# Attention over sorted edges: k and q[dst] both kept in SBUF, one block more ahead, and the weighing behind the logits

## The chip, the cores and the metric

The kernel runs on one core of one Trainium2 chip. The metric is the device time of one execution in microseconds, the median of several runs. The five engines of the core take their instructions each from a queue of its own and meet by semaphores: TensorE (PE, matrix products and transposes, into PSUM), VectorE (DVE), ScalarE (ACT), GpSimd (POOL, here the indirect loads) and SyncE (SP, here the other loads and stores).

## The reference, cut to what matters

There are N = 12500 nodes and E = 212500 edges of F = 128 numbers each, in 8 heads of 16. The edges come sorted by dst.

```
h = relu(layernorm(x))
q = h @ Wq.T + bq
k = edge_attr @ Wk.T + bk
v = h @ Wv.T + bv
qs, qd = q[src], q[dst]
in_m   = sum(qs * k)      # per edge and head
out_m  = sum(qd * k)
diag_m = sum(qs * qd)
att = edge_weight ** lam
score = (softmax_by_dst(in_m / 4) + softmax_by_dst(out_m / 4) + softmax_by_dst(diag_m / 4)) * att
out = x + leaky_relu(segment_sum(score * v[dst], dst) @ Wo.T + bo, 0.1)
```

So each edge needs the rows q[src], q[dst] and k, three products of them summed over a head, and then a softmax over the edges of one dst.

## The kernel before

The kernel first computes q for all nodes into a table in DRAM (some 160 us), then runs a loop over blocks of 512 edges, and ends with the output of the last nodes. The loop has 415 blocks. They belong to five streams, each a fifth of the sorted edges: block g is of stream s = g % 5 and turn t = g // 5, so a turn is five blocks, one of each stream. A block is four tiles of 128 edges (`JN` = 4).

For each block, in the order of the code:

- `gather` (GpSimd, L696): four indirect loads of q[src] into the tile `qq`, `LOOK` = 23 blocks ahead of their use, in `QQ` = 25 buffers. Each waits, besides its buffer, for a TensorE product noted in `behind`.
- `spread_q` (TensorE, L1201): since the edges are sorted, the dst of a block lie in a window of 38 nodes. One-hot columns (`oh`) times the window's rows of q (`win`, kept as three bf16 terms) give q[dst] in one half of the PSUM tile `kq_ps`, and the bias of k in the other half. `kq_ps` has two buffers of two banks each.
- `project` (TensorE, L1190): the turned edges `eT` times Wk are added to k's half of `kq_ps`. Behind it ScalarE copies the half with q[dst] to the SBUF tile `qd` (L1194).
- `turn` (TensorE, L1183): the next edges are transposed into `eT_ps` (one buffer), and ScalarE copies them to `eT` (L1185).
- `logits` (VectorE): q[dst] times k (L1215, from `qd` and `kq_ps`), then q[src] times both halves of `kq_ps` (L1216), into the tile `prod`. After the blocks s = 0, 2 and 4 the sums over the heads follow (L1220, of one block or of two) into `lT`.
- `one_hots` (ScalarE, L1177 and L1178): makes `oh` from the loaded positions `relb`.

Once per turn, spread over its five blocks, the work on the logits of earlier turns runs: `turn_logits` (L1241, transposes into `l_ps`), scans along the edges that give the maximum of each dst (L1274, L1279, L1292), `turn_max` (L1366, back into `m_ps`), `powers` at s = 3 (VectorE subtracts the maximum, L1376, and ScalarE takes the exponential, L1377, in the tile `back`), `show_ends` at s = 3 (L1402, L1405, L1406: the matrix `sel` of which edge belongs to which node), `weigh_powers` at s = 4 (VectorE, L1387: powers times the edges' weights, into the other half of `back`), and `to_rows` at s = 4 (L1417: `sel` times `back` into `w_ps`, and ScalarE's copy L1423). SyncE loads a turn's edges with one DMA (`fetch_edges`, L684, into `ea`, two buffers), its positions (`fetch_places`, L641, `relb`), the windows (`fetch_rows`, L650), the marks of the ends (`fetch`, L627, `far`), and stores the rows (`put_rows`, L1434). The class `Nodes` puts the output work of finished nodes between.

The order on each engine is fixed by hand: `pin` chains each instruction to the one that the code issued before it on the same engine. So the order of the lines in the loop is the order of work, and an instruction that waits holds all behind it on its engine. In block g the loop spreads and projects block g + 1, turns block g + 2, makes the one-hot columns of block g + 3 and multiplies block g.

Of the kernel before, what the change touches and what calls it, by code (L numbers as in the profile page):

```python
# [7 lines left out]
F32 = mybir.dt.float32  # L8
# [464 lines left out]
def ordered_path(ctx: ExitStack, tc: tile.TileContext, flag, x, src, dst, edge_attr, edge_weight,  # L473
# [19 lines left out]
    nc = tc.nc  # L493
    N, F = x.shape
    E = src.shape[0]
    P = 128
    NI = -(-N // P)
    NP = P * NI
    BE, JN = 512, 4
# [11 lines left out]
    H3 = 3 * HEADS  # L511
# [75 lines left out]
    worst = consts.tile([RW, 1], F32, name="worst")  # L587
    LEAD, RAW, AHEAD = 3, 15, 11
    raw_i = consts.tile([P, LEAD, S, JN], I32, name="raw_i")
    LOOK, QQ, BEGIN = 23, 25, 12  # L590
    end = S * G
    edges = ctx.enter_context(ExitStack())
    gath = edges.enter_context(tc.tile_pool(name="gath", bufs=QQ))
# [4 lines left out]
    def pin(inst):  # L598

        engine = str(inst.ins.engine)  # L600
        if engine in pinned:
            tc.add_manual_dep(inst.ins, pinned[engine], mybir.DependencyInfo(
                mybir.DependencyClass.NoSync, mybir.DependencyReason.DATA), reason="in order")
        pinned[engine] = inst.ins.name
        return inst
# [8 lines left out]
    qqs, st, eas, behind, base_v, places = {}, {}, {}, {}, {}, {}  # L614
# [29 lines left out]
    def fetch_rows(t, of=range(S)):  # L644
        if t >= G:
            return
        if 0 in of:
            st[t]["win"] = wins[t % 2]
        for s in of:
            win = pin(nc.sync.dma_start(st[t]["win"][:, s, :],  # L650
                                        q3_table[bass.ds(base_v[t][s] * 3, K3), :]))
            apart(win, [term_stores[u] for u in units_of(s, t)])
# [28 lines left out]
    def fetch_edges(t):  # L681
        if t < G:
            ea = eas[t] = load.tile([P, S, JN * F], F32, name="ea")
            pin(nc.sync.dma_start(  # L684
                ea, edge_attr[:end * BE, :].rearrange("(s b p j) f -> p s b (j f)", s=S, b=G, p=P)
                [:, :, t, :]))
# [52 lines left out]
    with tc.tile_pool(name="prep", bufs=1) as prep, \  # L739
# [44 lines left out]
        rest = E - (RW - 1) * RC  # L784
# [280 lines left out]
    class Nodes:  # L1065
# [39 lines left out]
        def turn(self, to):  # L1105
            for b in range(self.n):
                pin(nc.tensor.transpose(to[:, b, :], self.h[:, b, :], ident))
            if self.hT is None:
                self.hT = fin.tile([P, JN, P], F32, name="hT")
            pin(nc.scalar.copy(self.hT[:, :self.n], to[:, :self.n]))  # L1110
# [50 lines left out]
    with tc.tile_pool(name="work", bufs=2) as work, \  # L1161
            tc.tile_pool(name="scan", bufs=2) as scan, \
            tc.tile_pool(name="ps", bufs=1, space=PSUM) as ps:
        kqs, eTs, qds, ohs, lTs, prods = {}, {}, {}, {}, {}, {}

        def banks_of(g):

# [4 lines left out]
        def one_hots(g):  # L1172

            if g < end:
                oh = ohs[g] = work.tile([K3, BE], BF, name="oh", bufs=5)
                d = places[g // S][:K3, g % S, :]
                pin(nc.scalar.activation(d, d, AF.Abs, bias=before[:K3]))  # L1177
                pin(nc.scalar.activation(oh, d, AF.Relu, bias=1.0, scale=-1.0))  # L1178
# [9 lines left out]
        def project(g):  # L1188
            for j in range(JN):
                pin(nc.tensor.matmul(kqs[g][:, j, 1, :], eTs[g][:, j, :], wk, start=False,  # L1190
                                     stop=(j % 2 == 1)))
            del eTs[g]
            qds[g] = work.tile([P, JN, F], F32, name="qd")
            pin(nc.scalar.copy(qds[g], kqs[g][:, :, 0, :]))  # L1194

        def spread_q(g):

            s, win = g % S, st[g // S]["win"]
            kq = banks_of(g)
            for j in range(JN):  # L1200
                pin(nc.tensor.matmul(kq[:, j].rearrange("p i f -> p (i f)"),  # L1201
                                     ohs[g][:, j * P:(j + 1) * P], win[:, s:S + 1:S - s, :],
                                     start=(j % 2 == 0), stop=False))
            del ohs[g]

        def logits(g):
            s, t = g % S, g // S
            if s == 0:
                lTs[t] = scan.tile([P, JN, S, H3], F32, name="lT", bufs=3)
            alone = t == G - 1 and s > 2  # L1210
            lo = s if alone else max(0, s - 1 + s % 2)
            if s == lo:
                prods[0] = work.tile([P, JN, 2, 3, F], F32, name="prod", bufs=1)
            prod = prods[0][:, :, s - lo]
            pin(nc.vector.tensor_mul(prod[:, :, 2, :], qds[g], kqs[g][:, :, 1, :]))  # L1215
            pin(nc.vector.tensor_mul(prod[:, :, 0:2, :],  # L1216
                                     qqs[g][:, :, None, :].to_broadcast([P, JN, 2, F]),
                                     kqs[g]))
            if s % 2 == 0 or alone:
                pin(nc.vector.tensor_reduce(  # L1220
                    lTs[t][:, :, lo:s + 1, :].rearrange("p j s c -> p j (s c)"),
                    prods[0][:, :, :s + 1 - lo].rearrange("p j s i (h d) -> p j (s i h) d", d=DIM),
                    AX.X, ALU.add))
            del kqs[g], qds[g], qqs[g]

        last = {}
        ends_ab = scan.tile([P, len(rest) * JN, 2, 2 * H3], F32, name="ends_ab", bufs=1)
        for i in range(2):
            ends_t.append(scan.tile([K4, P], BF, name=f"ends_t{i + 2}", bufs=1))
            nc.vector.memset(ends_t[-1][0:1, :], 1.0)  # L1230
# [1 line left out]
        def small(shape, name):  # L1232
            return ps.tile(shape, F32, name=name, tag="small", bufs=3)
# [286 lines left out]

        products = str(mybir.EngineType.PE)
        leaving, last_pair = pairs[G - 3], pairs[G - 1]
        fetch_rows(0)
        fetch(1)
        fetch_places(1)
# [5 lines left out]
        turn(1)  # L1531
        one_hots(1)
        one_hots(2)
        for g in range(end):
            s, t = g % S, g // S
            nodes_before(t, s)
            gather(g + LOOK)
            if s == 0:
                fetch_edges(t + 1)
            if g + 1 < end:  # L1540
                spread_q(g + 1)
                behind[g + 1, 0] = pinned[products]
                project(g + 1)
                behind[g + 1, 1] = pinned[products]
            if g + 2 < end:
                turn(g + 2)
                behind[g + 1, 2] = pinned[products]
            if s == 4:
                later(weigh_powers, t - 2)
            logits(g)  # L1550
            if s == 3:
                later(powers, t - 2)
            one_hots(g + 3)
            if s == 0:
                if t > 0:
                    turn_logits(t - 1)
                later(select, t - 2)
                later(spread_far, t - 2)
            elif s == 1:
                later(scan_on, t - 1)  # L1560
                later(scan_back, t - 2)
                if t == 1:
                    logits_few()
            elif s == 2:
                if t == G - 2:
                    show_ends(G - 1)
                later(turn_max, t - 2)
                fetch_places(t + 2)
            elif s == 3:
                later(show_ends, t - 2)  # L1570
                fetch(t + 2)
            elif t < G - 1:
                later(to_rows, t - 2)
            ahead, k = (t + 2, s - 3) if s > 2 else (t + 1, s + 2)
            if ahead > 1:
                fetch_rows(ahead, [k])
            if g < end - 1:
                later(put_rows, t - 2 if s == 4 else t - 3, [(s + 1) % S])
            if t == G - 3 and 0 < s < 3:
                select(G - 2 + s)  # L1580
            if t == G - 2 and s == 4:
                show_ends(G)
            if t == G - 1 and s == 0:
                select(G - 2)
            if t == G - 1 and s == 4:
                show_ends(G - 2)
            behind[g + 1, 3] = pinned[products]
            nodes_between(t, s)
            other_terms(t, s)
            if g == 12 * S:  # L1590
                examine()
            begin_rest(g - (end - BEGIN))
            if g == end - 2:
                hold(rest[0], True)
            if g == end - 1:
                last_pair.turn(small([P, JN, P], "node_ps"))
                more_banks()
            if g < S:
                of = [u for u in range(NU) if g in parts_of(u)]
                pin(nc.scalar.dma_start(  # L1600
                    sums[g][of[0] * UN:(of[0] + len(of)) * UN].rearrange(
                        "(n p) i c -> p n (i c)", p=P),
                    blank[:, None, :].to_broadcast([P, 2 * len(of), 2 * 2 * H3])))
# [28 lines left out]
        hold(rest[1])  # L1632
        last_pair.turn(small([P, JN, P], "node_ps"))
        last_pair.project_o(small([P, JN, F], "node_ps"))
        for r, of in enumerate(rest):
            of.load_sums(ends_ab[:, r * JN:r * JN + of.n], of.more)
        last_pair.take_larger()
# [88 lines left out]
```

## Time and profile before

| what | us |
|---|---|
| three runs, median (lowest to highest) | 2659.78 (2658.79 to 2670.84) |
| the profiled execution, its own time | 2642.74 |
| its span, first to last instruction | 2640.9 |
| TensorE products, busy | 1657.0 (63%) |
| TensorE weight loads, busy (beside products) | 1406.9 (53%) |
| VectorE busy | 2002.2 (76%) |
| ScalarE busy | 1422.5 (54%) |
| GpSimd busy | 1587.3 (60%) |
| mean granted TensorE clock | 0.786 |
| moved by DMA | 355.74 MB, 135 GB/s on average |

The costliest groups of instructions besides those shown in the prediction, with their total, the mean of one, and the engine's idle time just before them:

```
L1190 TensorE  kq_ps, 4 a block      x3320  627.3 us, 348 ns   677.0 us idle before
L1220 VectorE  sums over the heads   x250   702.3 us, 2809 ns    8.5 us
L1185 ScalarE  copy of eT            x415   244.5 us, 589 ns   174.8 us
L1177 ScalarE  one-hot, first part   x415   301.8 us, 727 ns     0.0 us
L1178 ScalarE  one-hot, second part  x415   261.5 us, 630 ns    13.2 us
```

A matmul on f32 operands is shown as two passes, so 4 tiles of 415 blocks are 3320 records at L1190. Busy time is an average over the span. Which engine is waited for is read from the idle times before the groups and from the chain of waits, which follows the work that ended last back to the start. A waiter's releaser "remote" is one that the profile could not tie to an instruction. Ends of matmuls are modelled, not measured.

### The profile page before, as it was taken

The page shows a single profiled execution, that of the slowest core. Times are in us where ns is not written, and L with a number is a line of the kernel's source. Part 1 is how long each engine was busy: PE and PEld are TensorE (multiplying, and loading weights), DVE is VectorE, ACT ScalarE, POOL GpSimd, SP SyncE. Part 2 cuts the span into 40 slices and gives each one's busy share as a digit, 9 for nine tenths or more (in the row PEclk, how much of TensorE's full clock was granted, in tenths as well). Part 3 has the DMA queues.
Part 4 walks back from the last instruction along what each step waited for, and adds up shares of the span by engine and source line. Part 5 has one row for each costly group of instructions (what it writes and reads, how often), then busy time and mean ns, then how long its engine had stood idle before and what let it go on. Part 6 is the DMA issues. An engine that isn't in the chain of part 4 may idle for free.

```text
span 2640.9 us, 34648 instructions
## 1 busy us (share of the span) xinstructions
PE 1657.0 (63%) x9986; PEld 1406.9 (53%) x9986; DVE 2002.2 (76%) x2205; ACT 1422.5 (54%) x2742; POOL 1587.3 (60%) x1678
## 2 busy tenths in 40 slices
PE   5655656565665566666666666565666666666677
PEld 4544545454555455555555565454555555555665
DVE  6656777777787777777878777777877787778896
ACT  6644555455555555555555555555554555555572
POOL 6666666666666666666666666666666666666200
PEclk9876777778777887877878777878877787778786
DMA  8464444444444444444444444444444444444431
GB/s 235 143 202 130 132 121 121 145 131 121 129 147 132 131 132 148 140 132 130 134 139 144 126 134 144 144 122 130 146 139 129 124 145 139 120 126 133 122 91 53
DMA packets 306303, 355.74 MB, mean 135 GB/s; under 512 B 118433, under 2 KB 225899, under 8 KB 305795
## 3 DMA queue, kind: packets, MB, share of 16 engines
q1 hardware_dynamic: 238340, 238.99, 29.8%
q0 software_dynamic: 53184, 108.92, 15.0%
q10 hardware_dynamic: 14580, 5.53, 0.8%
q8 instruction: 82, 1.34, 0.2%
q14 instruction: 117, 0.96, 0.1%
HBM read 321.41 MB, written 31.85 MB: 134 GB/s over the span
## 4 chain that ended last, share of the span: by engine, by line
PE 31%; ACT 22%; another core or an unknown queue 17%; issue 14%; DVE 10%; DMA 0%; DVEq 0%; POOL 0%; ACTq 0%; SPq 0%; POOLq 0%
PE kq_ps L1190 11%; PE w_ps L1417 6%; PE kq_ps L1201 5%; ACT qd L1194 4%; ACT eT L1185 4%; PE eT_ps L1183 4%; ACT relb L1177 4%; DVE lT L1220 3%; DVE prod L1216 3%; ACT oh L1178 2%; PE node_ps L1115 2%; ACT sel L1406 2%; ACT sel L1405 2%; ACT back L1377 1%
## 5 line engine op out<-in xcount | busy, mean ns | idle before, releaser
L696 POOL DMA_INDIRECT qq<-q_table,src_i x1600 | 1517.2, 948 | 852.1 <-issue 368.8
L1190 PE MATMUL kq_ps<-wk,eT 128*128 128x128 f32 x3320 | 627.3, 348 | 677.0 <-ACT eT L1185 478.3
L1190 PEld LDWEIGHTS kq_ps<-wk,eT 128*128 128x128 f32 x3320 | 554.3, 252 | 757.7 <-ACT eT L1185 526.3
L1220 DVE TENSOR_REDUCE lT<-prod 128x192 f32<-128x3072 f32 (+1 forms) x250 | 702.3, 2809 | 8.5
L1194 ACT COPY qd<-kq_ps 128x512 f32<-128x512 f32 x415 | 242.0, 583 | 723.2 <-remote 443.9
L1216 DVE TENSOR_TENSOR prod<-qq,kq_ps 128x1024 f32<-128x1024 f32 x415 | 504.0, 1214 | 0.0
L1215 DVE TENSOR_TENSOR prod<-qd,kq_ps 128x512 f32<-128x512 f32 x415 | 283.1, 682 | 179.5 <-issue 97.5
L1201 PE MATMUL kq_ps<-win,oh 114*128 114x256 bf16 x1660 | 296.5, 307 | 96.8 <-issue 44.5
L1185 ACT COPY eT<-eT_ps 128x512 f32<-128x512 f32 x415 | 244.5, 589 | 174.8 <-remote 117.0
L1183 PE MATMUL eT_ps<-ident,ea 128*128 128x128 f32 x1660 | 321.4, 329 | 5.6 <-issue 5.6
L1177 ACT ACTIVATE relb<-relb,before 114x512 bf16<-114x512 bf16 x415 | 301.8, 727 | 0.0
L1201 PEld LDWEIGHTS <-oh 114*128 114x128 bf16 x1660 | 178.1, 111 | 172.6 <-issue 136.8
L1178 ACT ACTIVATE oh<-relb 114x512 bf16<-114x512 bf16 x415 | 261.5, 630 | 13.2
L1183 PEld LDWEIGHTS eT_ps<-ident,ea 128*128 128x128 f32 x1660 | 258.8, 175 | 6.2 <-issue 6.2
L1417 PE MATMUL w_ps<-back,sel 128*114 128x144 f32 (+1 forms) x1312 | 208.6, 323 | 72.4 <-ACT sel L1406 52.7
L1387 DVE TENSOR_TENSOR back<-back,m_ps 128x480 f32<-128x480 f32 x84 | 54.9, 653 | 256.1 <-ACT back L1377 239.3
L1417 PEld LDWEIGHTS w_ps<-back,sel 128*114 128x114 f32 x1312 | 194.3, 219 | 99.4 <-ACT sel L1406 72.7
L1274 DVE TENSOR_TENSOR_SCAN u<-far,u,l_ps 120x512 f32<-120x512 bf16 x82 | 104.5, 1275 | 30.0 <-PE kq_ps L1201 12.4
L1292 DVE TENSOR_TENSOR_SCAN m<-far_ps,head,u 120x512 f32<-120x512 f32 x81 | 103.9, 1282 | 8.4
L1423 ACT COPY rows<-w_ps 114x240 f32<-114x240 f32 x84 | 29.8, 355 | 129.1 <-PE kq_ps L1201 43.3
L696 POOL DMA_INDIRECT qq<-in_x_dram,raw_i x60 | 61.5, 1024 | 35.7 <-issue 15.6
L1366 PE MATMUL m_ps<-ident,m 120*128 120x120 f32 x332 | 70.1, 351 | 5.5 <-DVE m L1292 2.8
(196 smaller groups left out, 1458.8 us busy)
## 6 DMA issues: line engine op xcount, KB each, us to landing
ea<-in_edge_attr_dram SPq DMA_DIRECT2D x83, 1280.0 KB
relb<-rel_d SPq DMA_DIRECT2D x83, 640.0 KB
qq<-q_table,src_i POOLq DMA_INDIRECT x1600
win<-q_table SPq DMA_DIRECT2D x415, 28.5 KB
far<-far_d SPq DMA_DIRECT2D x84, 120.2 KB
q_table<-more_q SPq DMA_DIRECT2D x40, 192.0 KB
sums<-rows SPq DMA_DIRECT2D x408, 7.1 KB
q_table<-xq SPq DMA_DIRECT2D x24, 256.0 KB
```

Of the source, the lines that this page charges most:

```text
L696: rows = pin(nc.gpsimd.indirect_dma_start(out=qq[:, j, :], out_offset=None, in_=x if g < RAW else q_table, in_offset=bass.IndirectOffsetOn ...
L1177: pin(nc.scalar.activation(d, d, AF.Abs, bias=before[:K3]))
L1178: pin(nc.scalar.activation(oh, d, AF.Relu, bias=1.0, scale=-1.0))
L1183: pin(nc.tensor.transpose(eT_ps[:, j, :], eas[g // S][:, g % S, j * F:(j + 1) * F], ident))
L1185: pin(nc.scalar.copy(eT, eT_ps))
L1190: pin(nc.tensor.matmul(kqs[g][:, j, 1, :], eTs[g][:, j, :], wk, start=False, stop=(j % 2 == 1)))
L1194: pin(nc.scalar.copy(qds[g], kqs[g][:, :, 0, :]))
L1201: pin(nc.tensor.matmul(kq[:, j].rearrange("p i f -> p (i f)"), ohs[g][:, j * P:(j + 1) * P], win[:, s:S + 1:S - s, :], start=(j % 2 == 0), ...
L1215: pin(nc.vector.tensor_mul(prod[:, :, 2, :], qds[g], kqs[g][:, :, 1, :]))
L1216: pin(nc.vector.tensor_mul(prod[:, :, 0:2, :], qqs[g][:, :, None, :].to_broadcast([P, JN, 2, F]), kqs[g]))
L1220: pin(nc.vector.tensor_reduce(lTs[t][:, :, lo:s + 1, :].rearrange("p j s c -> p j (s c)"), prods[0][:, :, :s + 1 - lo].rearrange("p j s i ...
L1417: pin(nc.tensor.matmul(w_ps[:, own[0]:own[-1] + 1, :].rearrange("p s c -> p (s c)"), d["sel"][:n, j, lo:lo + TRIO, :].rearrange("p s w -> ...
```

## The change

`project` copies the whole of `kq_ps`, q[dst] and k, to an SBUF tile `kq` with three buffers, and drops its hold on the PSUM tile there. `logits` reads both factors from `kq`. TensorE's work moves one block ahead: in block g the loop now spreads and projects block g + 2, turns block g + 3 and makes the one-hot columns of block g + 4; ahead of the loop stands one more of each. `fetch_edges` is issued at s = 3 for the turn after the next, where it was at s = 0 for the next turn. `logits` of a block now stands ahead of `weigh_powers`. `LOOK` and `QQ` are one smaller, and `ends_ab`, used at the very end, takes the place of `prod` and no tile of its own.

```
-    LOOK, QQ, BEGIN = 23, 25, 12
+    LOOK, QQ, BEGIN = 22, 24, 12
...
         def project(g):
...
             del eTs[g]
-            qds[g] = work.tile([P, JN, F], F32, name="qd")
-            pin(nc.scalar.copy(qds[g], kqs[g][:, :, 0, :]))
+            held_kq[g] = work.tile([P, JN, 2, F], F32, name="kq", bufs=3)
+            pin(nc.scalar.copy(held_kq[g], kqs.pop(g)))
...
-            pin(nc.vector.tensor_mul(prod[:, :, 2, :], qds[g], kqs[g][:, :, 1, :]))
+            kq = held_kq.pop(g)
+            pin(nc.vector.tensor_mul(prod[:, :, 2, :], kq[:, :, 0, :], kq[:, :, 1, :]))
             pin(nc.vector.tensor_mul(prod[:, :, 0:2, :],
-                                     qqs[g][:, :, None, :].to_broadcast([P, JN, 2, F]),
-                                     kqs[g]))
+                                     qqs[g][:, :, None, :].to_broadcast([P, JN, 2, F]), kq))
...
+        fetch_edges(1)
         fetch_rows(0)
...
         one_hots(2)
+        spread_q(1)
+        project(1)
+        turn(2)
+        one_hots(3)
         for g in range(end):
             s, t = g % S, g // S
             nodes_before(t, s)
             gather(g + LOOK)
-            if s == 0:
-                fetch_edges(t + 1)
-            if g + 1 < end:
-                spread_q(g + 1)
+            if s == 3:
+                fetch_edges(t + 2)
+            if g + 2 < end:
+                spread_q(g + 2)
                 behind[g + 1, 0] = pinned[products]
-                project(g + 1)
+                project(g + 2)
                 behind[g + 1, 1] = pinned[products]
-            if g + 2 < end:
-                turn(g + 2)
+            if g + 3 < end:
+                turn(g + 3)
                 behind[g + 1, 2] = pinned[products]
+            logits(g)
             if s == 4:
                 later(weigh_powers, t - 2)
-            logits(g)
             if s == 3:
                 later(powers, t - 2)
-            one_hots(g + 3)
+            one_hots(g + 4)
```

The orders below show what this moves. The first is VectorE's, from the products of block s = 3 to the sums of block s = 4 of one turn: `prod` takes the products, `back` the powers, and `more_q` is a part of the table of q in work. Before:

```order
L1215 TENSOR_TENSOR prod<-qd,kq_ps 128x4x128
L1216 TENSOR_TENSOR prod<-qq,kq_ps 128x4x256
L1376 TENSOR_TENSOR back<-lT,m_ps 128x20x24
L1319 TENSOR_TENSOR more_q<-more_q,more_q_11360 128x256
L1387 TENSOR_TENSOR back<-back,m_ps 128x20x24
L1215 TENSOR_TENSOR prod<-qd,kq_ps 128x4x128
L1216 TENSOR_TENSOR prod<-qq,kq_ps 128x4x256
L1220 TENSOR_REDUCE lT<-prod 128x4x48
```

And in the changed kernel, whose line numbers there are one or two off:

```order
L1216 TENSOR_TENSOR prod<-kq 128x4x128
L1217 TENSOR_TENSOR prod<-qq,kq 128x4x256
L1375 TENSOR_TENSOR back<-lT,m_ps 128x20x24
L1318 TENSOR_TENSOR more_q<-more_q,more_q_11375 128x256
L1216 TENSOR_TENSOR prod<-kq 128x4x128
L1217 TENSOR_TENSOR prod<-qq,kq 128x4x256
L1220 TENSOR_REDUCE lT<-prod 128x4x48
L1386 TENSOR_TENSOR back<-back,m_ps 128x20x24
```

The product of powers and weights has moved behind the two products and the sums of its block, and the products read no PSUM tile any more.

The second place is ScalarE's queue at the exponential of the 40th turn with one (s = 3). Before:

```order
L1194 COPY qd<-kq_ps 128x512
L1185 COPY eT<-eT_ps 128x512
L1377 ACTIVATE back<-back 128x20x24
L1177 ACTIVATE relb<-relb,before 114x512
L1178 ACTIVATE oh<-relb 114x512
L1405 ACTIVATE sel<-d_ps 128x380 x2
L1406 ACTIVATE sel<-sel 128x760
```

And in the changed kernel:

```order
L1194 COPY kq<-kq_ps 128x1024
L1185 COPY eT<-eT_ps 128x512
L1376 ACTIVATE back<-back 128x20x24
L1177 ACTIVATE relb<-relb,before 114x512
L1178 ACTIVATE oh<-relb 114x512
L1404 ACTIVATE sel<-d_ps 128x380 x2
L1405 ACTIVATE sel<-sel 128x760
```

The rows stand as before, but the copy is twice as long, and the block that is copied and turned there is one later: 210 copies of L1194 stand ahead of this exponential before, 211 now. VectorE's difference, for which the exponential waits, stands behind the products of the same block as before.

The third place is SyncE's queue around the load of a turn's edges (`ea`); the rows called ISA set the address of the DMA behind them. Before:

```order
L1434 ISA
L1434 DMA sums_67<-rows 38x48
L684 DMA ea<-in_edge_attr_dram 128x5x512
L1393 DMA ends_t_103<-rel_d 20x1x128
L650 ISA
L650 DMA win_108<-q_table 114x128
```

And in the changed kernel:

```order
L641 DMA relb<-rel_d 128x5x512
L650 ISA
L650 DMA win_107<-q_table 114x128
L1433 ISA
L1433 DMA sums_70<-rows 38x48
L684 DMA ea<-in_edge_attr_dram 128x5x512
L627 DMA far<-far_d 120x1x513
L629 TENSOR_LOAD bases
```

The load of edges has moved from the start of a turn to s = 3 of the turn ahead of it, behind the load of positions and ahead of `far`.

More of the change, by code (lines that the diff above doesn't have):

```diff
@@ L1163, in ordered_path @@
             tc.tile_pool(name="ps", bufs=1, space=PSUM) as ps:
-        kqs, eTs, qds, ohs, lTs, prods = {}, {}, {}, {}, {}, {}
+        kqs, eTs, held_kq, ohs, lTs, prods = {}, {}, {}, {}, {}, {}
         def banks_of(g):
@@ L1223, in logits @@
                     AX.X, ALU.add))
-            del kqs[g], qds[g], qqs[g]
+            del qqs[g]
         last = {}
-        ends_ab = scan.tile([P, len(rest) * JN, 2, 2 * H3], F32, name="ends_ab", bufs=1)
         for i in range(2):
@@ L1634, in ordered_path @@
         last_pair.project_o(small([P, JN, F], "node_ps"))
+        ends_ab = work.tile([P, JN, 2, 3, F], F32, name="prod", bufs=1).rearrange(
+            "p j s i f -> p (j s i f)")[:, :len(rest) * JN * 4 * H3].rearrange(
+            "p (n i c) -> p n i c", i=2, c=2 * H3)
         for r, of in enumerate(rest):
```

## The prediction

> **What bounds the kernel now.** I read the busy times by stage first, to see whether one engine is full.
>
> ```profile
> core 0: us, PE busy (x) PEld busy (x) DVE busy (x) ACT busy (x) POOL busy (x), PEclk, DMA share, GB/s
> 200.00:1300.00 1100.00, 677.14 (x4087) 577.00 (x4088) 835.68 (x787) 579.51 (x1092) 706.54 (x746) 0.78 0.45 133
> 2470.00:2585.00 115.00, 82.04 (x538) 70.76 (x536) 106.13 (x99) 82.47 (x163) 3.91 (x7) 0.85 0.32 98
> ```
>
> None is. In the loop (200 to 1300 us) VectorE works 76% of the time, GpSimd 64%, TensorE 62%, ScalarE 53%. After 2470 us, when the gathers of q[src] are all issued, VectorE reaches 92%. So for most of the run something else than an engine's own work sets the pace. Next I read the pace itself, from the first and the last start of a product, and the last gather.
>
> ```profile
> L1215 DVE TENSOR_TENSOR prod<-qd,kq_ps x415: 659/687/690, 162.1 to 2584.8; 128x512 f32<-128x512 f32 x139
> L696 POOL DMA_INDIRECT qq<-q_table,src_i x1600: 942/947/1900, 101.4 to 2471.9; - x178
> ```
>
> The 415 blocks start from 162.1 to 2584.8: (2584.8 - 162.1) / 414 = 5.85 us a block. VectorE's work is 0.76 x 5.85 = 4.45 us of that. The chain of waits says who fills the rest.
>
> ```profile
> span 2640.9 us, 34648 instructions
> PE 31%; ACT 22%; another core or an unknown queue 17%; issue 14%; DVE 10%; DMA 0%; DVEq 0%; POOL 0%; ACTq 0%; SPq 0%; POOLq 0%
> PE kq_ps L1190 11%; PE w_ps L1417 6%; PE kq_ps L1201 5%; ACT qd L1194 4%; ACT eT L1185 4%; PE eT_ps L1183 4%; ACT relb L1177 4%; DVE lT L1220 3%; DVE prod L1216 3%; ACT oh L1178 2%; PE node_ps L1115 2%; ACT sel L1406 2%; ACT sel L1405 2%; ACT back L1377 1%
> ```
>
> VectorE holds a tenth of the chain. Over half lies on TensorE and ScalarE, and 17% on something unknown. A stretch of the timeline shows the ring that these two form.
>
> ```profile
> 1202.88 1.93 PE L1190 MATMUL kq_ps<-wk,eT 128*128 128x128 f32 x8
> 1204.65 0.60 PE L1183 MATMUL eT_ps<-ident,ea 128*128 128x128 f32 x4
> 1206.09 0.60 PE L1201 MATMUL kq_ps<-win,oh 114*128 114x256 bf16 x4 [0.37 <-DVE prod L1216]
> 1208.51 0.59 ACT L1194 COPY qd<-kq_ps 128x512 f32<-128x512 f32 x1 [4.40 <-remote]
> 1212.09 0.59 ACT L1185 COPY eT<-eT_ps 128x512 f32<-128x512 f32 x1 [2.99 <-remote]
> 1212.73 2.08 PE L1190 MATMUL kq_ps<-wk,eT 128*128 128x128 f32 x8 [6.04 <-ACT eT L1185]
> ```
>
> The projection of one block (L1190) and the turn of the next block's edges (L1183) are shown as ended by 1205.3. Yet ScalarE's copies, which wait for nothing but these two products (and an old buffer), start at 1208.5 and 1212.1, and the next projection waits 6 us for the copied eT. So the shown ends of TensorE run ahead of the moment at which others may read, by several us, and this delay sits inside the ring projection, copy of q[dst], copy of eT, next projection. It is the "unknown" of the chain. What causes it I can't read from the trace. It goes with the gathers: ScalarE's wait before L1194 is 691.7 us for 385 blocks before 2470 us and 12.2 us for 23 blocks after.
>
> ```profile
> L1194 ACT COPY qd<-kq_ps 128x512 f32<-128x512 f32 x385 | 224.6, 583 | 691.7 <-remote 433.6 <-PE kq_ps L1201 96.4 <-PE kq_ps L1190 51.5
> L1194 ACT COPY qd<-kq_ps 128x512 f32<-128x512 f32 x23 | 13.4, 581 | 12.2 <-PE kq_ps L1190 10.6 <-remote 0.9 <-issue 0.4
> ```
>
> That is 1.80 us a block against 0.53. The ring is the bound, and the change doesn't touch its delay.
>
> **The longer copy.** L1194 now copies 1024 elements a partition out of PSUM where it copied 512. Three copies out of PSUM of other lengths give the price.
>
> ```profile
> L1423 ACT COPY rows<-w_ps 114x240 f32<-114x240 f32 x84 | 29.8, 355 | 129.1 <-PE kq_ps L1201 43.3 <-PE w_ps L1417 28.8 <-remote 17.1
> L1405 ACT ACTIVATE sel<-d_ps 128x380 f32<-128x380 f32 x164 | 69.7, 475 | 0.1
> L1194 ACT COPY qd<-kq_ps 128x512 f32<-128x512 f32 x415 | 242.0, 583 | 723.2 <-remote 443.9 <-PE kq_ps L1201 96.4 <-PE kq_ps L1190 63.7
> ```
>
> (583 - 355) / (512 - 240) = 0.84 ns an element, and the middle row fits (355 + 140 x 0.84 = 473, shown 475). So 583 + 512 x 0.84 = 1012 ns: 0.43 us more, 415 times, 178 us of ScalarE's time. What of it lies on the path? ScalarE issues the copy of kq and then that of eT, for which the next projection waits, so each us of the first delays the second unless the turn is late anyway, as at 1212.09 above. The chain holds 4% of 2640.9 = 106 us of L1194, which is 106 / 0.583 = 181 copies. 181 x 0.43 = **78 us added**. Bounds: 0, if a late turn hides them all, and 178, if none; I take the chain's share.
>
> **What uncoupling from VectorE takes away.** Now q[dst] and k of a block leave PSUM by that copy, so the banks come free when ScalarE has copied, not when VectorE has multiplied, and TensorE works two blocks ahead of VectorE instead of one. Gone is the wait of the spread of q (L1201) for VectorE's product two blocks back. Eased is the wait of ScalarE's exponential (L1377) for VectorE's difference.
>
> ```profile
> L1201 PE MATMUL kq_ps<-win,oh 114*128 114x256 bf16 x1660 | 296.5, 307 | 96.8 <-issue 44.5 <-DVE prod L1216 42.9 <-ACT oh L1178 5.9
> ACT back L1377 <- DVE back L1376: 14.2, 5, 4.9
> L1387 DVE TENSOR_TENSOR back<-back,m_ps 128x480 f32<-128x480 f32 x83 | 54.2, 654 | 255.4 <-ACT back L1377 239.3 <-issue 10.8 <-ACT eT L1185 5.4
> ```
>
> 42.9 + 14.2 = **57 us taken away**. Bounds: 0, since a projection that waits for eT gains nothing from an earlier spread, and 57 + 44.5 = 102, if the unnamed waits of L1201 are VectorE's too.
>
> **The product of powers and weights.** L1387 loses nearly its whole wait of 239 us, because the sum of logits, 5.2 us of work, now stands ahead of it. That is time of an engine that is off the chain for 90% of the span; alone it is worth 0. What follows it is w_ps on TensorE.
>
> ```profile
> 1216.82 0.66 DVE L1387 TENSOR_TENSOR back<-back,m_ps 128x480 f32<-128x480 f32 x1 [2.09 <-ACT back L1377]
> 1217.39 0.68 DVE L1215 TENSOR_TENSOR prod<-qd,kq_ps 128x512 f32<-128x512 f32 x1
> 1217.98 1.22 DVE L1216 TENSOR_TENSOR prod<-qq,kq_ps 128x1024 f32<-128x1024 f32 x1
> 1218.84 0.84 ACT L1406 ACTIVATE sel<-sel 128x760 f32<-128x760 f32 x1
> 1219.23 3.35 DVE L1220 TENSOR_REDUCE lT<-prod 128x192 f32<-128x3072 f32 x1
> 1219.73 0.50 PE L1417 MATMUL w_ps<-back,sel 128*114 128x144 f32 x2 [0.58 <-issue]
> ```
>
> L1387 ends at 1217.5 and w_ps starts at 1219.73, after sel: 2.2 us to spare. Moved behind 5.2 us of work, with the 2.09 us of waiting saved, it would be 5.2 - 2.1 - 2.2 = 0.9 us late, 83 x 0.9 = 75 us at worst. Queued behind a waiting w_ps on TensorE are the next spread and projection. I take 0, because VectorE needs 4.45 us a block and the ring 5.85, so VectorE has caught up by the time TensorE is there.
>
> **The rest.** VectorE's products now read both operands from SBUF.
>
> ```profile
> L1216 DVE TENSOR_TENSOR prod<-qq,kq_ps 128x1024 f32<-128x1024 f32 x415 | 504.0, 1214 | 0.0
> L1215 DVE TENSOR_TENSOR prod<-qd,kq_ps 128x512 f32<-128x512 f32 x415 | 283.1, 682 | 179.5 <-issue 97.5
> L1319 DVE TENSOR_TENSOR more_q<-more_q,more_q 128x256 f32<-128x256 f32 x40 | 16.8, 419 | 5.7 <-issue 4.4 <-ACT more_q L1317 1.4
> ea<-in_edge_attr_dram SPq DMA_DIRECT2D x83, 1280.0 KB
> GB/s 235 143 202 130 132 121 121 145 131 121 129 147 132 131 132 148 140 132 130 134 139 144 126 134 144 144 122 130 146 139 129 124 145 139 120 126 133 122 91 53
> ```
>
> L1216 and L1215 give (1214 - 682) / 512 = 1.04 ns an element and 150 ns fixed; L1319, which reads SBUF alone, has 419 - 256 x 1.04 = 153 fixed. So they cost the same: 0. The look-ahead of the gathers counts one block less from a point one block earlier: 0. SP issues the load of edges three blocks later in the turn but for the turn after, so it lands earlier against its need, and it now stands right behind the load of relb; its bytes are the same: 0. Ahead of the loop stand one more spread, projection and turn, and a load of 1280 KB ahead of the first windows: between 0 and 5.6 us (1280 KB at 235 GB/s, the fastest slice above); I take 0.
>
> **Sum.** 2642.7 (the profiled execution) + 78 - 57 = 2664. The median of the runs is 17 us above the profiled one, so I put the difference on it: 2659.8 + 21 = **2681 us**.
>
> **Rivals.**
> *They cancel or hide each other.* If two thirds of the copies hide behind a late turn, the change is worth 26 - 57 = -31 to about +13 us: 2647 to 2673, within the 0.5% (13 us) that a measurement of this kernel tells from no change. For it: 17% of the chain is the delay, behind which a copy may hide.
>
> *The lead pays.* All 102 us go and every copy hides: 2558; half of that, 2608. For it: the last 115 us, where VectorE runs at 92% once nothing holds the ring. Against it: the rows above name only 57 us of waiting for VectorE, and a ring that has more room is no shorter.
>
> *It gets no further ahead.* The ring paces TensorE, so nothing of the 57 is gained, and only the copy is paid: 2738.
>
> *GpSimd becomes the bound.* Both products now read two operands from SBUF. A gather that starts inside such an operation of today is stretched.
>
> ```profile
> 743.21 0.42 DVE L1319 TENSOR_TENSOR more_q<-more_q,more_q 128x256 f32<-128x256 f32 x1
> 741.99 0.94 POOL L696 DMA_INDIRECT qq<-q_table,src_i  x1 [0.30 <-issue]
> 743.24 1.20 POOL L696 DMA_INDIRECT qq<-q_table,src_i  x1 [0.30 <-issue]
> ```
>
> The gather that began 0.03 us into L1319 took 0.26 us longer: it was held until about 0.13 us before the operation's end. The Trainium skill (SBUF — State Buffer, section Who interferes with whom) has this as a rule: a VectorE instruction with two SBUF inputs contends with a GpSimd instruction that reads SBUF, and the later one blocks until the first ends. By that rule the time would be the one worked out here, and this gather agrees with it. The two products fill 1.8 us of each block (0.6 + 1.2, rows above), so a gather can be held for 0 to 1.7 us once a block. Unhindered, four gathers take 4 x 1.25 = 5.0 us (starts 741.99 and 743.24). With a start each 1.25 us, one falls 0 to 1.25 us into the pair, which holds it 1.07 us on average: 6.07 us a block, and the 392 blocks gathered in the loop end at 162 + 392 x 6.07 = 2541, still ahead of 2585. It decides from (2585 - 162) / 392 = 6.18 us a block on, a hold of 1.17. At 1.7 each time the end is 2788, 203 us later; halfway between, 80 us later: 2740. Against it: the average doesn't reach. But it caps the gain of the rival before at 2585 - 2541 = 44 us.
>
> **Chances.** The forecast, a small loss between 2674 and 2730: 0.33. Cancelled: 0.19. The lead pays, 2558 to 2646: 0.30. No further ahead: 0.10. GpSimd: 0.08. So faster 0.30, same 0.19, slower 0.51. The range 2590 to 2765 leaves out a third of the faster case and the far end of GpSimd's (worst w_ps and worst copies, 2660 + 75 + 178, lie beyond it too). The likeliest case alone has 2674 to 2730.
>
> **What would show it.** L1194 near 1012 ns and a larger share of the chain; L1201 no longer waiting for VectorE; L1387's line without its wait; the unknown share of the chain unchanged near 17%; gathers longer than 948 ns on average. I am wrong if the unknown delay shrinks, if ScalarE's longer copy is on the chain no oftener than before, or if the last gather comes later than the last block allows.

## The result and the profile after

| | median us | runs from | to | ratio to before, 95% interval |
|---|---|---|---|---|
| before | 2659.28 | 2655.03 | 2670.84 | |
| changed | 2702.67 | 2699.24 | 2712.51 | 1.0163 (1.0128 to 1.0197) |

The change made the kernel slower by 43 us. The page of the changed kernel has, against the rows shown of before (engine, operation, count, total and mean of one; then the engine's idle time just before the group and what ended most of it):

```profile
span 2703.1 us, 34116 instructions
PE 1655.5 (61%) x9986; PEld 1412.7 (52%) x9986; DVE 1997.4 (74%) x2205; ACT 1591.7 (59%) x2742; POOL 1767.4 (65%) x1678
L696 POOL DMA_INDIRECT qq<-q_table,src_i x1600 | 1697.6, 1061 | 732.2 <-issue 385.4
L1190 PE MATMUL kq_ps<-wk,eT 128*128 128x128 f32 x3320 | 616.9, 344 | 747.5 <-ACT eT L1185 397.1
L1194 ACT COPY kq<-kq_ps 128x1024 f32<-128x1024 f32 x415 | 418.7, 1009 | 709.8 <-remote 429.2
L1216 DVE TENSOR_TENSOR prod<-kq 128x512 f32<-128x512 f32 x415 | 283.4, 683 | 29.9 <-ACT kq L1194 13.9
L1217 DVE TENSOR_TENSOR prod<-qq,kq 128x1024 f32<-128x1024 f32 x415 | 505.5, 1218 | 0.0
L1201 PE MATMUL kq_ps<-win,oh 114*128 114x256 bf16 x1660 | 295.6, 308 | 2.8 <-ACT oh L1178 2.0
L1416 PE MATMUL w_ps<-back,sel 128*114 128x144 f32 (+1 forms) x1312 | 233.1, 350 | 163.4 <-DVE back L1386 69.3
```

The same groups of before that are not shown above:

```profile
L696 POOL DMA_INDIRECT qq<-q_table,src_i x1600 | 1517.2, 948 | 852.1 <-issue 368.8
L1190 PE MATMUL kq_ps<-wk,eT 128*128 128x128 f32 x3320 | 627.3, 348 | 677.0 <-ACT eT L1185 478.3 <-issue 186.8 <-ACT qd L1194 11.3
L1417 PE MATMUL w_ps<-back,sel 128*114 128x144 f32 x656 | 132.8, 359 | 72.4 <-ACT sel L1406 52.7 <-issue 11.0 <-ACT sel L1405 6.9
```

The copy L1194 has become 1009 ns long, as worked out, and L1201's wait has fallen from 96.8 us to 2.8. But L1190, the next product on TensorE, now waits 747.5 us where it waited 677.0. The gathers take 1061 ns where they took 948. And w_ps (L1416) waits 163.4 us where it waited 72.4. The groups of the changed kernel's trace with all releasers of their idle time show for whom:

```profile
L1190 PE MATMUL kq_ps<-wk,eT 128*128 128x128 f32 x3320 | 616.9, 344 | 747.5 <-ACT eT L1185 397.1 <-issue 306.5 <-ACT kq L1194 43.5
L1416 PE MATMUL w_ps<-back,sel 128*114 128x144 f32 x656 | 143.3, 381 | 163.4 <-DVE back L1386 69.3 <-DVE lT L1220 35.8 <-ACT sel L1405 20.0
L1386 DVE TENSOR_TENSOR back<-back,m_ps 128x480 f32<-128x480 f32 x83 | 53.6, 646 | 18.5 <-ACT back L1376 8.8 <-issue 8.1 <-ACT eT L1185 1.6
L1376 ACT ACTIVATE back<-back 128x480 f32<-128x480 f32 x83 | 50.8, 612 | 18.6 <-DVE back L1375 15.3 <-issue 3.1
```

VectorE idles 18.5 us before the product of powers and weights (L1386) where it idled 255.4, and TensorE has got a wait instead: 69.3 us for that product and 35.8 us for the sums ahead of it. VectorE has not gained that time: it idles 174.1 us before the scan L1273 (30.0 before) and 149.8 us before the difference L1375 (18.9 before). The exponential waits for VectorE as long as before (15.3 us, 14.2 before). The chain of waits of this execution breaks off after less than half of the span, so I show that of another execution of the same kernel (w2_after, below):

```profile
PE 30%; ACT 22%; another core or an unknown queue 15%; issue 15%; DVE 13%; POOL 3%; DMA 1%; ACTq 0%; DVEq 0%; SPq 0%; POOLq 0%
PE kq_ps L1190 9%; ACT kq L1194 8%; PE w_ps L1416 8%; PE kq_ps L1201 5%; DVE lT L1220 4%; ACT eT L1185 3%; PE eT_ps L1183 3%; ACT relb L1177 3%; DVE prod L1217 3%; POOL qq L696 3%; PE node_ps L1115 1%; DVE prod L1216 1%; ACT oh L1178 1%; ACT sel L1405 1%
```

TensorE and ScalarE hold over half of it as before, VectorE 13% (10% before), and the unknown part is 15%, 17% before.

A stretch of the timeline shows a held gather (start, length, engine, instruction):

```profile
1204.44 0.67 DVE L1216 TENSOR_TENSOR prod<-kq 128x512 f32<-128x512 f32 x1
1205.02 1.22 DVE L1217 TENSOR_TENSOR prod<-qq,kq 128x1024 f32<-128x1024 f32 x1
1205.31 1.75 POOL L696 DMA_INDIRECT qq<-q_table,src_i  x1 [0.31 <-issue]
1207.36 0.94 POOL L696 DMA_INDIRECT qq<-q_table,src_i  x1 [0.30 <-issue]
```

The gather that began 0.29 us into the second product took 1.75 us, so it was held until about 0.1 us before the product's end; the next one, beside the sums, took 0.94.

### The profile page after: what moved, and what is told of

It is laid out like the page before. It is cut to its first block, busy times and chain, and to the rows that moved or that the text cites. A ratio compares the mean times of both kernels' runs of the same rounds, so it can differ in the third digit from the quotient of the medians.

```text
span 2703.1 us, 34116 instructions
## 1 busy us (share of the span) xinstructions
PE 1655.5 (61%) x9986; PEld 1412.7 (52%) x9986; DVE 1997.4 (74%) x2205; ACT 1591.7 (59%) x2742; POOL 1767.4 (65%) x1678
## 3 DMA queue, kind: packets, MB, share of 16 engines
q0 software_dynamic: 53184, 108.92, 15.3%
## 5 line engine op out<-in xcount | busy, mean ns | idle before, releaser
L696 POOL DMA_INDIRECT qq<-q_table,src_i x1600 | 1697.6, 1061 | 732.2 <-issue 385.4
L1190 PE MATMUL kq_ps<-wk,eT 128*128 128x128 f32 x3320 | 616.9, 344 | 747.5 <-ACT eT L1185 397.1
L1190 PEld LDWEIGHTS kq_ps<-wk,eT 128*128 128x128 f32 x3320 | 541.4, 247 | 835.4 <-ACT eT L1185 442.4
L1194 ACT COPY kq<-kq_ps 128x1024 f32<-128x1024 f32 x415 | 418.7, 1009 | 709.8 <-remote 429.2
L1217 DVE TENSOR_TENSOR prod<-qq,kq 128x1024 f32<-128x1024 f32 x415 | 505.5, 1218 | 0.0
L1416 PE MATMUL w_ps<-back,sel 128*114 128x144 f32 (+1 forms) x1312 | 233.1, 350 | 163.4 <-DVE back L1386 69.3
L1416 PEld LDWEIGHTS w_ps<-back,sel 128*114 128x114 f32 x1312 | 218.9, 243 | 188.3 <-issue 61.2
L1216 DVE TENSOR_TENSOR prod<-kq 128x512 f32<-128x512 f32 x415 | 283.4, 683 | 29.9 <-ACT kq L1194 13.9
L1201 PE MATMUL kq_ps<-win,oh 114*128 114x256 bf16 x1660 | 295.6, 308 | 2.8 <-ACT oh L1178 2.0
L1273 DVE TENSOR_TENSOR_SCAN u<-far,u,l_ps 120x512 f32<-120x512 bf16 x82 | 104.8, 1277 | 174.1 <-remote 69.5
L1201 PEld LDWEIGHTS <-oh 114*128 114x128 bf16 x1660 | 177.9, 112 | 80.6 <-issue 44.0
L1375 DVE TENSOR_TENSOR back<-lT,m_ps 128x480 f32<-128x480 f32 x83 | 54.1, 651 | 149.8 <-issue 62.2
L1123 DVE TENSOR_TENSOR h<-node_ps,score 128x512 f32<-128x512 f32 x19 | 13.1, 691 | 113.1 <-PE node_ps L1115 77.4
```

Source lines behind the costliest of these rows:

```text
L696: rows = pin(nc.gpsimd.indirect_dma_start(out=qq[:, j, :], out_offset=None, in_=x if g < RAW else q_table, in_offset=bass.IndirectOffsetOn ...
L1194: pin(nc.scalar.copy(held_kq[g], kqs.pop(g)))
L1216: pin(nc.vector.tensor_mul(prod[:, :, 2, :], kq[:, :, 0, :], kq[:, :, 1, :]))
L1217: pin(nc.vector.tensor_mul(prod[:, :, 0:2, :], qqs[g][:, :, None, :].to_broadcast([P, JN, 2, F]), kq))
L1416: pin(nc.tensor.matmul(w_ps[:, own[0]:own[-1] + 1, :].rearrange("p s c -> p (s c)"), d["sel"][:n, j, lo:lo + TRIO, :].rearrange("p s w -> ...
```

## The experiments

The runs fell on several chips, and the chips differ. On three of them before took 2637 to 2662 us, as in the result above; on two it took 2160. I call the first the late chips, because their profiles show TensorE's ends seen late, and the others the prompt chips. Ratios are always to before, run in turn with it on the same chip. Theories: *copy* (the step that my forecast paid for), *weighing* (its new place holds TensorE), *GpSimd* (gathers held by VectorE's reads of SBUF), *delay* (the late ends come from the gathers), and later *lead* (working one block ahead helps once gathers don't bind).

### One part at a time

The long copy alone: before, with the copy of 1024 elements, while VectorE still takes k from PSUM. `LOOK`, `QQ` and the place of `ends_ab` are as in the changed kernel.

```
-            qds[g] = work.tile([P, JN, F], F32, name="qd")
-            pin(nc.scalar.copy(qds[g], kqs[g][:, :, 0, :]))
+            qds[g] = work.tile([P, JN, 2, F], F32, name="kq", bufs=3)
+            pin(nc.scalar.copy(qds[g], kqs[g]))
...
-            pin(nc.vector.tensor_mul(prod[:, :, 2, :], qds[g], kqs[g][:, :, 1, :]))
+            pin(nc.vector.tensor_mul(prod[:, :, 2, :], qds[g][:, :, 0, :], kqs[g][:, :, 1, :]))
```

> Before, with ScalarE's copy taken to 1024 elements (q[dst] and k go to SBUF), while VectorE still takes k from PSUM; look-ahead and buffers as in the changed kernel. Theory copy: 78 us slower than before (0 to 178), near 2737. Theory weighing (the late product of powers and weights holds TensorE): within 13 us of before. Theory GpSimd (gathers held by VectorE's SBUF reads): within 13 us, and gathers stay at 948 ns, since no product has two SBUF operands.

Then, on top of it, both products from SBUF (`kqs.pop(g)` at the copy, both factors from `qds[g]`), in the order of before:

> As the run with the long copy alone, but both products read q[dst] and k from SBUF and the PSUM banks are let go behind the copy; the order of work stays that of before. Theory copy: the 78 us of the copy stay and up to 57 us of waits for VectorE go, 2680 to 2737. Theory weighing: 2602 to 2660, no slower than before. Theory GpSimd: gathers near 1061 ns as in the changed kernel, and some 40 us slower than the run with the long copy alone.

The changed kernel with the weighing put back:

```
+            if s == 4:
+                later(weigh_powers, t - 2)
             logits(g)
-            if s == 4:
-                later(weigh_powers, t - 2)
```

> The changed kernel with the product of powers and weights put back ahead of the logits of its block. Theory copy: 2703 as the changed kernel, within 13 us. Theory weighing: w_ps no longer waits 69 us for that product (and 36 us for the sums ahead of it), 2600 to 2660. Theory GpSimd: 2703, gathers still near 1061 ns.

And before with the weighing alone moved behind, the same lines the other way round:

> Before, with only the product of powers and weights moved behind the logits of its block. Theory copy: within 13 us of before, 2659. Theory weighing: 40 to 75 us slower, 2700 to 2735, with w_ps waiting for that product. Theory GpSimd: within 13 us of before.

All four fell on a prompt chip, where before took 2159.79:

| | us | ratio |
|---|---|---|
| long copy alone | 2163.31 | 1.0019 (1.0008 to 1.0031) |
| and products from SBUF | 2377.57 | 1.1019 (1.0993 to 1.1044) |
| changed, weighing first | 2351.38 | 1.0892 (1.0869 to 1.0914) |
| before, weighing last | 2341.43 | 1.0841 (1.0818 to 1.0864) |

The times expected were for a late chip, so only differences compare. The copy costs 3.5 us there, not 78. The reads of SBUF and the late weighing each cost some 180 to 215 us, far more than any theory expected. The third row has the lead of one block and the earlier load of edges besides what the second has, and nothing else: these two together gain 26 us on this chip. For the reads, the line of the gathers says why, first with the long copy alone, then with products from SBUF (least, median and longest, and the first and the last start):

```profile
L696 POOL DMA_INDIRECT qq<-q_table,src_i x1600: 940/944/2358, 90.4 to 2094.6; - x178
```
```profile
L696 POOL DMA_INDIRECT qq<-q_table,src_i x1600: 940/945/3015, 89.1 to 2310.5; - x178
```

(2094.6 - 90.4) / 1600 = 1.25 us from gather to gather, 5.01 us a block; with products from SBUF 1.39 and 5.55. The second product of each block, which reads what was gathered (again long copy first):

```profile
L1216 DVE TENSOR_TENSOR prod<-qq,kq_ps x415: 1200/1214/1222, 120.6 to 2107.6; 128x1024 f32<-128x1024 f32 x139
...
  DMA qq<-q_table,src_i: 10.2, 6
```
```profile
L1216 DVE TENSOR_TENSOR prod<-qq,kq x415: 1205/1219/1289, 119.9 to 2320.0; 128x1024 f32<-128x1024 f32 x139
...
  DMA qq<-q_table,src_i: 181.1, 69
```

A block takes (2107.6 - 120.6) / 414 = 4.80 us with the copy alone: less than its gathers' 5.01, so the gathers' lead of some 20 blocks is used up slowly, and just lasts. At 5.55 it is gone sooner: VectorE's waits for gathered rows begin behind 500 us and come to 181.1 us. GpSimd is the bound, as its line with products from SBUF shows:

```profile
L696 POOL DMA_INDIRECT qq<-q_table,src_i x1600 | 1732.7, 1083 | 487.6 <-issue 275.1
```

The gathers alone take 1732.7 - 1515.2 = 218 us longer than with the long copy alone (its line stands in the last section), the idle time between them is the same, and the span grew by 213 us. For the late weighing, the waits of that run show TensorE behind VectorE (engine, line, for whom; total, times, longest):

```profile
PE w_ps L1417 <- DVE back L1387: 232.0, 59, 6.0
```

### The changed kernel again, and half of the gathers

The changed kernel itself, on a late chip:

> The changed kernel again, unaltered, beside before on the same chip. Where TensorE's ends are seen late (before near 2659), 1.016 times before. Where they are not (before near 2160): theory GpSimd, gathers at 1061 ns and 1.37 us a gather with its gap make 392 x 5.5 us = 2156 us of gathers behind the start at 120, so 2345 to 2400, no more than with the weighing put first, since the weighing hides in the wait for gathers; theory weighing, both losses add, 2500 to 2560.

It took 2702.93 against 2662.2: 1.0158 (1.0138 to 1.0179), as before. On the same chip, both kernels with half of their gathers (two of a block's four are left out, with their waits for TensorE's products, and the first gathered tile stands in for all four):

```
             for j in of:
+                if j > 1 and g >= RAW:
+                    continue
...
-                                     qqs[g][:, :, None, :].to_broadcast([P, JN, 2, F]),
+                                     qqs[g][:, 0:1, None, :].to_broadcast([P, JN, 2, F]),
```

> Before with half of the gathers left out (two of the four of each block), the first gathered tile standing in for q[src] of all four. Theory GpSimd: gathers do not bound before, so at most 2% faster than before. Theory delay (the late ends of TensorE come from gathers): where before takes near 2659, the unknown share of the chain of waits falls under 5% and the time below 2400.

> The changed kernel with the same half of its gathers left out. Theory GpSimd: held gathers no longer bound, so the loss against before with half of its gathers falls to what the late weighing costs, 0 to 13 us where VectorE catches up. Theory weighing: 80 to 180 us slower than before with half of its gathers. Theory copy: 20 to 78 us slower, with ScalarE's copy on the chain.

Before with half of its gathers took 2172.77 us, 0.8162 (0.8146 to 0.8178) of before on this late chip: almost the prompt chips' time with all gathers. Its busy times and its chain of waits:

```profile
PE 1539.1 (71%) x9986; PEld 1329.8 (61%) x9986; DVE 1988.4 (92%) x2205; ACT 1412.7 (65%) x2742; POOL 827.9 (38%) x878
DVE 59%; PE 12%; issue 11%; ACT 11%; DMA 3%; SPq 1%; another core or an unknown queue 1%; POOLq 0%; POOL 0%; DVEq 0%; ACTq 0%
```

The unknown part fell from 17% to 1%, and VectorE, a tenth of the chain before, holds 59% and is busy 92% of the span. So theory GpSimd's "at most 2%" fell, and theory delay held: on late chips the late ends go with the gathers. Whether it is the gathers themselves or the waits that hang on them isn't told apart. The changed kernel with half of its gathers took 2328.53, 156 us more, as theory weighing had it, with this wait:

```profile
PE w_ps L1418 <- DVE back L1388: 430.0, 78, 8.5
```

To see whether that is all of the 156 us, the weighing was put first there too, and in the changed kernel with all gathers:

> The changed kernel with the product of powers and weights put back ahead of its block's logits, all gathers in. Where TensorE's ends are seen late (before near 2660): theory weighing, the 43 us of loss go, 2645 to 2675; theory GpSimd, 2690 to 2715, since gathers stay near 1061 ns; theory copy, 2690 to 2715. Where they are not (before near 2160): 1.089 times before, as on that chip already.

> The changed kernel with half of its gathers left out (as in the run before it with half of them) and the product of powers and weights put back ahead. Theory weighing: the 156 us between the two kernels with half of their gathers go, 2160 to 2190. Theory copy: 80 us or more of them stay, 2250 and above. Theory lead (an uncoupled TensorE helps once gathers don't bind): below 2150.

These two fell on a prompt chip (before 2160.77). With all gathers: 2350.91, 1.0876 (1.0857 to 1.0894), the number of the other prompt chip again. With half: 2161.73, 0.9996 (0.9985 to 1.0007) of before with all of its gathers. Before with half of them was not run on that chip; on the late chip it took 2172.77, 0.5% more. VectorE is busy 92% of the span in that run on the late chip, and also on a prompt chip in the run with the long copy alone and all gathers, so before has little to gain there from fewer gathers. So with gathers out of the way, the longer copy, the reads of SBUF and the lead together come to nothing that these runs show, within that 0.5%, and the late weighing is the loss of 156 us.

### The same on late chips

> The changed kernel with the weighing put first, a third time, for a chip on which TensorE's ends are seen late (before near 2660): theory weighing, 2645 to 2675, level with before; theory GpSimd or copy, 2690 to 2715, level with the changed kernel. On a chip without that (before near 2160): 1.088 times before again.

> The changed kernel, unaltered. Before near 2660: 1.016 again. Before near 2160: if the late weighing hides behind the wait for held gathers, 2340 to 2400, within 2% of the run with the weighing first; if both losses add, 2500 to 2560.

A late chip: before 2657.29, weighing first 2682.87, 1.0091 (1.0070 to 1.0112), changed 2705.05, 1.0160 (1.0137 to 1.0182). Both theories missed: the weighing's place is worth 22 us, about half, and 26 us stay. With the weighing first, w_ps waits 91.4 us, nearer to the 72.4 of before, and no longer for VectorE:

```profile
L1416 PE MATMUL w_ps<-back,sel 128*114 128x144 f32 x656 | 130.2, 354 | 91.4 <-ACT sel L1405 53.4 <-issue 24.1 <-ACT sel L1404 12.1
```

The last run asked whether the copy is what stays:

> Before with the longer copy alone, again, for a chip on which TensorE's ends are seen late. There (before near 2660), theory copy: what is left of the loss once the weighing stands first, 20 to 30 us, is the copy's, so 2677 to 2690, and up to 2735 if uncoupling and lead give something back. Theory GpSimd or lead: the copy is free there too, 2650 to 2667. On a chip without late ends (before near 2160): 1.002 times before, as on such a chip already.

On another late chip before took 2637.26 and the long copy alone 2639.35: 1.0007 (0.9990 to 1.0023), so -3 to +6 us. The copy is free on late chips too. Its page:

```profile
PE 35%; ACT 22%; issue 16%; another core or an unknown queue 11%; DVE 7%; POOL 2%; DMA 1%; SPq 0%; DVEq 0%; ACTq 0%; POOLq 0%
PE kq_ps L1190 13%; ACT kq L1194 8%; PE w_ps L1416 6%; PE kq_ps L1201 6%; PE eT_ps L1183 5%; ACT eT L1185 4%; ACT relb L1177 3%; DVE lT L1220 3%; DVE prod L1216 3%; POOL qq L696 2%; PE node_ps L1115 1%; PE m_ps L1365 1%; ACT oh L1178 1%; ACT far_ps L1284 1%
L1194 ACT COPY kq<-kq_ps 128x1024 f32<-128x1024 f32 x415 | 418.7, 1009 | 615.9 <-remote 287.1
```

The copy's share of the chain rose from 4% to 8%, 0.08 x 2643 / 1.009 = 210 copies, while the unknown share fell from 17% to 11% and the wait ahead of the copy from 723.2 us to 615.9. That is 107 us of the 177 by which the copies grew; the longer copy seems to have taken most of its time out of the delay. (The two traces may be of different chips.)

## Why the prediction came out

The forecast, 21 us slower and slower more likely than not, had the right sign and the time lay within its range. That is luck: of the two terms that made the 21, the copy measured next to nothing and the uncoupling wasn't seen, and the loss came from terms that the text put at 0. The signs that it named came, all of them: a copy of 1009 ns with a larger share of the chain, L1201 and L1386 nearly without their waits, an unknown share of 14 to 15%, gathers of 1061 ns. They showed that the edit did what it should, and not that its parts were priced rightly.

- **The bound** was read rightly as far as TensorE's late ends go. That they go with the gathers, which the prediction had only from the stretch behind the last gather, is now shown by leaving half of them out; what causes the delay stays open. That the length of ScalarE's copy counts in a ring which sets the pace is not borne out: 177 us more of copying cost 2.
- **The longer copy: 78 us given, 2 measured** (-3 to +6). The instruction costs what was worked out, 1009 ns. The step that failed is "I take the chain's share": a share of the chain says who was last, not who is last once this one is longer. The prediction's own rival, that 17% of the chain is delay "behind which a copy may hide", describes what the run with the copy alone shows.
- **Uncoupling: 57 us given back, none of it seen.** L1201 lost its 94 us of waits, but L1190, behind it, waits 712 to 748 us in three executions of the changed kernel where it waited 677.0, and the exponential waits as before. That fits the lower bound that the text gave, "a projection that waits for eT gains nothing from an earlier spread", in part only: the wait named for eT fell from 478.3 to 397.1 us, and the one that nothing is named for rose from 186.8 to 306.5. With gathers halved the lead shows no gain. On a prompt chip, where GpSimd is the bound, the lead and the earlier load gain 26 us, with gathers of 1065 ns where they were 1083. On late chips it wasn't timed by itself.
- **The weighing: 0 given, 22 us measured** on a late chip, within the bound of 75. The failing step is "VectorE has caught up by the time TensorE is there". It takes the pace as even. But the unnamed wait at L1194, 443.9 us in all, stands before 101 of the 415 copies only, so TensorE is late in some blocks and prompt in others, and 21 times in 83 turns it stood before the product. Where TensorE is prompt throughout, VectorE (busy 92% before the move) seldom catches up: TensorE waits 78 times and the loss is 156 us with half of the gathers, 59 times and 182 us on a prompt chip.
- **The held gathers** were seen rightly (1061 ns against 948), and so was that they don't bind on the chip of the result: GpSimd idles 732.2 us ahead of them. Their size was not: 4 x (1061 - 948) = 0.45 us a block, where 1.07 was worked out for the average hold. The Trainium skill (SBUF — State Buffer, section Who interferes with whom) says that a VectorE instruction with two SBUF inputs contends with a GpSimd instruction that reads SBUF. The gathers of 946 to 948 ns where a product's factor is in PSUM, and of 1056 to 1083 where both are in SBUF, agree. The rival's point of decision, 6.18 us a block, was worked out from before's 5.85 us a block and holds for late chips alone. On a prompt chip a block takes 4.80 us, and there 5.55 us of held gathers are the bound, which costs 9 to 10%.
- **The rest: 0 given, about 24 us measured**, that is 2682.87 - 2657.29 less the 2 us of the copy. It lies in the reads of SBUF, the lead of one block and the earlier load of edges together. On late chips no run tells these apart. Since the late ends go with the gathers there, longer gathers may cost in that way without being the bound; that was not tried. Nor was the changed kernel timed on a prompt chip, so whether the late weighing and the held gathers add up there is not known.

So 2 + 24 + 22 = 48 us in that comparison, where 78 - 57 + 0 + 0 = 21 was forecast. No version with all of its gathers beats before. About half of the loss on late chips has a shown cause, the place of the weighing.

## What to carry to other kernels

Before an instruction of VectorE goes behind more work, look for who takes its result: here one product moved by 5.2 us of work holds TensorE's next matmul, and the argument that the engine has time on average hid it. A copy that frees PSUM also turns VectorE's operands into SBUF reads, and a gather that starts beside such a product is held; compare the gathers' time a block with the block's, as it would be on the quickest chip. And price an edit by making it alone: the chain's share of the copy doubled, and the time rose by 0.07%.

## What was not expected of the hardware

One kernel, unaltered, takes 2160 us on two chips and 2637 to 2662 on three others. The difference goes with the gathers: with half of them left out, the slower kind runs it in 2173. The granted clock is 0.78 to 0.80 on the late chips and 0.81 to 0.83 on the prompt ones, but it isn't what makes the difference: one execution of before on a late chip was granted 0.597 and took 2650.1 us. On the late chips ScalarE waits where the profile shows the products of TensorE as ended several us before, 443.9 us in total at L1194 without a releaser named; on a prompt chip TensorE's own product is named in that line instead, with the long copy alone:

```profile
L696 POOL DMA_INDIRECT qq<-q_table,src_i x1600 | 1515.2, 947 | 487.7 <-issue 249.7
L1194 ACT COPY kq<-kq_ps 128x1024 f32<-128x1024 f32 x415 | 417.7, 1007 | 227.4 <-PE kq_ps L1190 212.1
```

The gathers themselves are equally long on both, 948 and 947 ns. By what way they, or the waits that hang on them, delay TensorE there stays open.
